# Layer 1's queries and output projections as single products of 128 array columns

## The chip, the cores and the metric

The kernel runs on one core of a Trainium2 chip. The metric is the device time of one execution in microseconds, taken several times; times are compared by their median. A profile is one more execution, recorded by the hardware profiler: every instruction with its engine, its start and its length. The engines are TensorE (PE; its weight loads are listed apart as PEld), VectorE (DVE), ScalarE (ACT), GpSimd (POOL) and SyncE (SP), whose queue issues most of the DMAs.

## What is computed

Two post-norm transformer layers over 8 sequences of 512 tokens with 512 features, all in f32. The part that matters here is the attention of layer 1, with 8 query heads of 64 features and 2 heads of keys and values:

```python
h = norm_scale * x / (nrm + EPS) * split_scale
q = (h @ Wq.T).reshape(b, s, H, dh)          # H = 8, dh = 64
k = (h @ Wk.T).reshape(b, s, G, dh)          # G = 2
v = (h @ Wv.T).reshape(b, s, G, dh)
...
scores = jnp.einsum('bghsd,bgtd->bghst', q, k) / np.float32(np.sqrt(dh))
attn = jax.nn.softmax(scores, axis=-1)
out = jnp.einsum('bghst,bgtd->bghsd', attn, v)
out = out.reshape(b, H, s, dh).transpose(0, 2, 1, 3).reshape(b, s, H * dh)
return x + out @ Wo.T
```

Ahead of it stand layer 0's causal attention with 16 heads and a mixture of 8 experts of which each token takes 2; behind it a gated feed-forward with integer weights of 1408 hidden units. A layer norm follows each of the four parts. The change touches layer 1's attention alone.

## The kernel before

The program runs in four stages: layer 0's attention, the experts' tiles (128 tokens each), layer 1's attention, layer 1's feed-forward. All 8 sequences ("batches" b) go through one stage before the next one begins, apart from a few pieces that are drawn forward at the seams.

Layer 1's attention is the class `Attention1`. A batch is held turned, features on the partitions: `hT` is 128 partitions by 4 blocks c of 128 features by 512 tokens. The query heads are paired, one head of each group of keys beside one of the other: a pair g (of 4) has 2 x 64 = 128 columns. The pieces of work, with the lines that the profile names them by:

- `key`, `value` (L1746, L1754): the 128 columns of both heads' keys or values. The results are `ps_k` and `ps_v`.
- `query(g)` (L1763): the 128 columns of the pair g, four products over the feature blocks c, summed in one PSUM bank `ps_q`, and a copy by ScalarE to `qT` (L1770).
- `score` (L1869): for 128 keys at a time, the scores of both heads of a pair against 512 queries (`sc`), four products with 64 rows and 64 columns; ScalarE then writes the exponentials `p` (L1876).
- `product` (L1888): `p` with the values, summed over the four blocks of keys in `av` (L1895); one product of 64 columns for each head.
- `normalise` (L1900): the sums over the keys by a product with ones, `rs` (L1903), then ScalarE's copy (L1081), VectorE's reciprocal (L1906) and multiplication (L1913) into `aoT`, the attention's turned result.
- `project(b, t)` (L1835) and `project_groups` (L1841): the output projection of 128 tokens t, four products over the pairs of heads, into `ps_o`; VectorE adds it to the stream (L1848).

The products of keys, values, queries and outputs all go through `multiply` (L1713), which hands them to `matmul_by_columns` (L61). That one cuts a product of 128 columns of weights into products of `columns` columns each, which write their own part of the partitions of the result; every one of them reads the whole moving operand. All instructions that it makes have the line L65 in the profile, so the tile's name (`ps_q`, `ps_o`, `ps_k`, `ps_v`, `sc`) tells them apart. The first argument of `multiply` chooses: where it is zero (or false) the product stays whole, with 128 columns; else it is cut in two of 64. Keys and values pass b, queries `b or g`, outputs 1. So before the change only batch 0's keys, values and the query of its pair 0 are whole.

A product of f32 operands in the program stands as two instructions on TensorE, each with its weight load.

The order of the work is written out: `batches` (L1808) takes, for each batch, eight slots from `plan` (L1916). In each slot TensorE gets the scores of two units (a unit is a pair g and a block of keys), then the pieces that the plan has put there (queries, keys, values, outputs of the batch before, transposes), then `product` for the two units of the slot before, and after every fourth unit `normalise`. TensorE, VectorE, ScalarE and GpSimd run their instructions in this order (`in_order`, L68), and the DMAs of this stage are issued from the same pieces. Queries come in slots 0, 1, 3 and 7 in the middle batches (slot 7's is the first of the next batch, behind its values), outputs in slots 2 to 5. Batch 7 has in four slots a piece that turns a block of batch 0 for the feed-forward with transposes (`ps_xT`, L1196). After the last slot come batch 7's own outputs: the first three products of token block 0, `rs`, three products of each of the other token blocks, and the fourth products of all four, each followed by VectorE's L1848. Then the feed-forward begins with `ps_g` (L1231); its banks were in part those of the scores and outputs.

Of the kernel before, what the change touches and what calls it, by code (L numbers as in the profile page):

```python
# [18 lines left out]
P = 128  # L19
# [1674 lines left out]
class Attention1:  # L1694
# [21 lines left out]
    def prepare(self, b):  # L1716


        nc, own, w_qkv = self.nc, self.own, self.w_qkv
        st = self.state[b] = {"qT": [None] * ND}  # L1720
        combine = Combine(self.router, b, self.rows, ("rows0", "rows1"))

        def norm():
            st["xn"], st["scale"] = combine.norm()

        def turn(c):
            if c == 0:
                st["hT"] = own.tile([P, ND, S], F32, tag="hT", name="hT1")
            ps = self.mm([P, S], "ps_hT")
            for t in range(NT):  # L1730
                nc.tensor.transpose(ps[:, ts(t, P)], st["xn"][:, t, ts(c, P)], self.env.ident)
            nc.scalar.copy(st["hT"][:, c, :], ps)

        def blocks(t):
            if t == 0:
                st["room"] = self.rows.tile([P, ND * S], F32, tag="rows1", name="turned")
            self.turn.blocks(st["room"], t, st["xn"][:, t, :])
            if t == NT - 1:
                self.turn.out(st["room"])
                st["hT"] = own.tile([P, ND, S], F32, tag="hT", name="hT1")  # L1740
                back = self.turn.back(st["hT"].rearrange("p k s -> p (k s)"))
                if 2 <= b < NB - 1:
                    with self.env.tc.issue_after(back.ins):
                        self.load_rows(b + 1)

        def key():  # L1746
            hT = st["hT"]
            ps = self.mm([P, S], "ps_k1")
            for c in range(ND):
                self.multiply(b, ps, w_qkv[:, 4, ts(c, P)], hT[:, c, :], c)  # L1750
            st["kT"] = own.tile([P, S], F32, tag="kT", name="kT", bufs=2)
            nc.scalar.copy(st["kT"], ps)

        def value():  # L1754
            hT = st["hT"]
            ps = self.mm([P, NT, P], "ps_v1")
            for t in range(NT):
                for c in range(ND):
                    self.multiply(b, ps[:, t, :], hT[:, c, ts(t, P)], w_qkv[:, 5, ts(c, P)], c)
            st["v"] = own.tile([P, NT, P], F32, tag="v", name="v1", bufs=2)  # L1760
            nc.scalar.copy(st["v"], ps)

        def query(g):  # L1763

            hT = st["hT"]
            ps = self.mm([P, S], "ps_q1")
            for c in range(ND):
                self.multiply(b or g, ps, w_qkv[:, c, ts(g, P)], hT[:, c, :], c)
            st["qT"][g] = (self.work if g % 2 else own).tile([P, S], F32, tag="qT", name="qT")
            nc.scalar.copy(st["qT"][g], ps)  # L1770

        return {"fetch": combine.fetch, "add": combine.add, "sum": combine.sum, "stat": combine.stat, "deviations": combine.deviations, "norm": norm,
                "turn": turn, "blocks": blocks, "key": key, "value": value, "query": query}
# [34 lines left out]
    def batches(self, work, p_sc, p_av, weights, split):  # L1808
        env, nc, guard, state, HD = self.env, self.nc, self.guard, self.state, self.HD
# [6 lines left out]
        w_out = work.tile([P, ND, 512], F32, name="attn1_out")  # L1816
# [18 lines left out]
        def project(b, t):  # L1835
            ps = self.mm([P, D], "ps_o1")
            project_groups(b, t, ps, range(ND))
            residual(b, t, ps)
            statistics(b, t)

        def project_groups(b, t, ps, groups):  # L1841
            for c in groups:
                self.multiply(1, ps, state[b]["aoT"][:, c, ts(t, P)], w_out[:, c, :], c)

        def residual(b, t, ps):
            st = state[b]
# [22 lines left out]
        def score(b, g, kt):  # L1869
            st = state[b]  # L1870
            sc = p_sc.tile([P, 2, S], F32, tag="sc", name="sc1")
            for j in range(2):
                hs = slice(HD * j, HD * (j + 1))
                matmul_by_columns(nc, sc[:, j, :], st["kT"][hs, ts(kt, P)], st["qT"][g][hs, :], columns=HD)
            p = work.tile([P, 2, S], F32, tag="p", name="p1", bufs=4)
            nc.scalar.activation(p, sc, AF.Exp, scale=scale)  # L1876
            return p
# [87 lines left out]
        for b in range(NB):  # L1965
            for i, thunks in enumerate(plan(b)):
                units = [(b, u // NT, u % NT) for u in (2 * i, 2 * i + 1)]
                ps = [score(*unit) for unit in units]
# [12 lines left out]
        b = NB - 1  # L1981
        banks = [self.mm([P, D], "ps_o1")]
        project_groups(b, 0, banks[0], range(ND - 1))
        sums[-1]()
        prepare_table(AF.Silu)
        banks += [p_sc.tile([P, 2, S], F32, tag="sc", name="ps_o1")[:, 1, :] for _ in range(2)]
        banks.append(self.mm([P, D], "ps_o1"))
        for t in range(1, NT):
            project_groups(b, t, banks[t], range(ND - 1))
# [360 lines left out]
```

## Time and profile before

| | us |
|---|---|
| three runs | 2099.91, 2100.9, 2104.41 |
| their median | 2100.9 |
| the profiled execution | 2098.14 |
| its span, first to last instruction | 2096.2 |
| TensorE busy in the span | 2072.5 |
| VectorE, ScalarE, GpSimd busy | 1275.9, 606.8, 503.3 |

By stage, in us of the span:

| stretch | what | TensorE busy | VectorE busy |
|---|---|---|---|
| 0 to 716 | layer 0's attention, first tiles of the experts | 707.9 | 488.1 |
| 716 to 1057 | the experts' tiles | 339.8 | 110.5 |
| 1057 to 1600 | layer 1's attention | 540.9 | 428.2 |
| 1600 to 2096 | the feed-forward | 483.9 | 249.1 |

How to read a line of the groups: line of the kernel, engine, operation, result<-operands, rows\*columns of the array, shape and type of the moving operand, number of instructions, then busy time in us and the mean length of one in ns, and the idle time of the engine just before them. A line of the timeline has the start and the length of a merged run of instructions in us, then the same names and their number. Two matmuls on different columns of the array run side by side, so the busy time of a pair is that of one. The length of a single matmul includes its way through the array; what a stream of them costs is the distance of their starts.

### The profile page before, as it was taken

The page shows a single profiled execution, that of the slowest core. Times are in us where ns is not written, and L with a number is a line of the kernel's source. Part 1 is how long each engine was busy: PE and PEld are TensorE (multiplying, and loading weights), DVE is VectorE, ACT ScalarE, POOL GpSimd, SP SyncE. Part 2 cuts the span into 40 slices and gives each one's busy share as a digit, 9 for nine tenths or more (in the row PEclk, how much of TensorE's full clock was granted, in tenths as well). Part 3 has the DMA queues.
Part 4 walks back from the last instruction along what each step waited for, and adds up shares of the span by engine and source line. Part 5 has one row for each costly group of instructions (what it writes and reads, how often), then busy time and mean ns, then how long its engine had stood idle before and what let it go on. Part 6 is the DMA issues. An engine that isn't in the chain of part 4 may idle for free. (4 is left out here: it accounts for less than half of the span.)

```text
span 2096.2 us, 35861 instructions
## 1 busy us (share of the span) xinstructions
PE 2072.5 (99%) x15074; PEld 1048.4 (50%) x15074; DVE 1275.9 (61%) x1965; ACT 606.8 (29%) x840; POOL 503.3 (24%) x509
## 2 busy tenths in 40 slices
PE   9999999999999999999999999999999999999998
PEld 2333333333334677774433333333335888888886
DVE  2667776777768633234157888887868644455444
ACT  2333433324333111111143333333332322222222
POOL 1343444434433221221052231222101000000000
PEclk9999999999999999999999999999999999999999
DMA  9011304324233568876431332233102311111000
GB/s 327 22 46 57 102 16 117 122 70 154 82 102 112 171 200 256 243 225 203 148 101 51 121 111 81 66 106 101 41 1 71 101 41 61 61 61 61 20 21 22
DMA packets 182090, 213.39 MB, mean 102 GB/s; under 512 B 72586, under 2 KB 126090, under 8 KB 178850
## 3 DMA queue, kind: packets, MB, share of 16 engines
q1 hardware_dynamic: 169280, 172.85, 26.3%
q0 software_dynamic: 10560, 34.61, 5.7%
q10 hardware_dynamic: 2082, 3.56, 0.6%
q8 instruction: 121, 1.98, 0.4%
q14 instruction: 47, 0.39, 0.1%
HBM read 132.58 MB, written 78.40 MB: 101 GB/s over the span
## 5 line engine op out<-in xcount | busy, mean ns | idle before, releaser
L1492 ACT ACTIVATE p<-sc 128x2048 f32<-128x2048 f32 (+1 forms) x96 | 153.1, 1595 | 172.0 <-PE sc L65 148.3
L1236 DVE SCALAR_TENSOR_TENSOR hT<-ps_u,vec,sg 128x512 f32<-128x512 f32 x88 | 65.5, 745 | 190.1 <-PE ps_u L1231 189.9
L1084 POOL TENSOR_TENSOR g_total<-g_total,r_inv 128x512 f32<-128x512 f32 x64 | 90.7, 1417 | 351.8 <-DVE r_inv L1906 270.8
L1247 PE MATMUL ps_f<-ffn_w,h_half 128*128 128x512 f32 x664 | 167.7, 393 | 2.7 <-DVE h_half L1242 2.0
L964 PE MATMUL ps_gu<-xrT,experts 128*128 128x256 f32 x736 | 166.6, 379 | 0.0
L964 PEld LDWEIGHTS ps_gu<-xrT,experts 128*128 128x128 f32 x736 | 139.3, 190 | 35.9 <-issue 19.3
L1539 DVE TENSOR_TENSOR p<-p 128x1536 f32<-128x1536 f32 (+2 forms) x96 | 136.5, 1422 | 32.6 <-PE av L1531 17.6
L1502 POOL TENSOR_SCALAR_AFFINE_SELECT p<-p 128x512 f32<-128x512 f32 x128 | 84.4, 672 | 290.7 <-ACT p L1492 287.6
L1876 ACT ACTIVATE p<-sc 128x1024 f32<-128x1024 f32 x128 | 124.2, 1022 | 100.3 <-PE sc L65 99.0
L1906 DVE RECIPROCAL r_inv<-r_inv 128x512 f32<-128x512 f32 x32 | 107.1, 3347 | 72.7 <-ACT r_inv L1081 72.7
L1247 PEld LDWEIGHTS ps_f<-ffn_w,h_half 128*128 128x128 f32 x664 | 122.9, 188 | 34.4 <-DVE h_half L1242 7.3
L1231 PE MATMUL ps_g<-x_high,ffn_w 128*128 128x512 f32 x352 | 137.2, 390 | 0.0
L1231 PE MATMUL ps_g<-x_low,ffn_w 128*128 128x512 f32 x352 | 137.0, 389 | 0.0
L1231 PE MATMUL ps_u<-x_high,ffn_w 128*128 128x512 f32 x352 | 137.0, 389 | 0.0
L1231 PE MATMUL ps_u<-x_low,ffn_w 128*128 128x512 f32 x352 | 137.0, 389 | 0.0
L65 PE MATMUL sc<-qT,kT 64*64 64x512 f32 x1024 | 124.7, 602 | 1.2 <-ACT qT L1770 0.9
L65 PE MATMUL ps_q<-experts 128*32 128x512 f32 x1024 | 121.2, 602 | 4.7 <-DMA experts<-in_xT 4.4
L65 PE MATMUL ps_v<-experts 128*32 128x512 f32 x1024 | 120.9, 594 | 0.0
L1895 PE MATMUL av<-p,v 128*64 128x512 f32 x512 | 120.8, 593 | 0.0
L1234 ACT ACTIVATE sg<-ps_g,vec 128x512 f32<-128x512 f32 x88 | 60.6, 689 | 195.4 <-PE ps_g L1231 195.4
L65 PE MATMUL ps_o<-attn_out,aoT 128*64 128x512 f32 x512 | 116.4, 598 | 0.0
L65 PE MATMUL ps_k<-experts 128*32 128x512 f32 x1024 | 116.3, 594 | 0.0
(280 smaller groups left out, 3270.3 us busy)
## 6 DMA issues: line engine op xcount, KB each, us to landing
results<-y SPq DMA_DIRECT2D x68, 256.0 KB, 2.9
pair<-xrT SPq DMA_DIRECT2D x30, 512.0 KB, 3.0
xrT<-pair SPq DMA_DIRECT2D x120, 128.0 KB, 3.9
turned<-turned SPq DMA_DIRECT2D x56, 256.0 KB, 4.1
x<-in_x SPq DMA_DIRECT2D x8, 1024.0 KB, 8.5
rows<-x SPq DMA_DIRECT2D x32, 256.0 KB, 2.1
experts<-in_xT SPq DMA_DIRECT2D x7, 1024.0 KB, 11.8
x<-rows SPq DMA_DIRECT2D x14, 512.0 KB, 6.6
```

The lines of the kernel that those rows point to most:

```text
L65: nc.tensor.matmul(out[m], lhsT=lhsT[:, m], rhs=rhs, start=start, stop=stop)
L964: nc.tensor.matmul(ps[:, j, :], lhsT=w, rhs=xT[:, c, :], start=c == 0, stop=c == ND - 1)
L1084: self.nc.gpsimd.tensor_tensor(self.total, self.total, r_inv, ALU.add)
L1231: nc.tensor.matmul(ps, lhsT=w[:, ts(dc, P)], rhs=x[:, dc, :], start=(dc, i) == (0, 0), stop=(dc, i) == (ND - 1, 1))
L1236: nc.vector.scalar_tensor_tensor(hT, u, vec[:, V_SU + c : V_SU + c + 1], sg, ALU.mult, ALU.mult)
L1247: self.nc.tensor.matmul(os[t], lhsT=h[:, ts(t, P)], rhs=self.weights(2 * NHID + c), start=(c, i) == (0, 0), stop=(c, i) == (NHID - 1, 1))
L1492: nc.scalar.activation(p, sc[:, :, :width], AF.Exp, scale=scale)
L1502: select = nc.gpsimd.affine_select(out=first, in_=first, pattern=[[0, 4], [1, P]], compare_op=ALU.is_ge, fill=0.0, base=0, channel_multipl ...
L1539: nc.vector.tensor_tensor(total[:, :, P * kt :], total[:, :, P * kt :], p[:, :, at : at + w], ALU.add)
L1876: nc.scalar.activation(p, sc, AF.Exp, scale=scale)
L1895: nc.tensor.matmul(st["av"][HD * j : HD * (j + 1), :], lhsT=st["v"][:, kt, HD * j : HD * (j + 1)], rhs=p[:, j, :], start=kt == 0, stop=kt ...
L1906: nc.vector.reciprocal(r_inv, r_inv)
```

## The change

Queries and output projections pass 0 to `multiply` in place of `b or g` and 1. Each of their products is then a single one of 128 columns that reads its moving operand once; the results, their banks and the places in the order stay as they are. Keys and values are still cut in two for the batches after 0, the scores and the products with `p` and ones are as before.

```diff
@@ -1765,7 +1765,7 @@
             hT = st["hT"]
             ps = self.mm([P, S], "ps_q1")
             for c in range(ND):
-                self.multiply(b or g, ps, w_qkv[:, c, ts(g, P)], hT[:, c, :], c)
+                self.multiply(0, ps, w_qkv[:, c, ts(g, P)], hT[:, c, :], c)
             st["qT"][g] = (self.work if g % 2 else own).tile([P, S], F32, tag="qT", name="qT")
             nc.scalar.copy(st["qT"][g], ps)
 
@@ -1840,7 +1840,7 @@
 
         def project_groups(b, t, ps, groups):
             for c in groups:
-                self.multiply(1, ps, state[b]["aoT"][:, c, ts(t, P)], w_out[:, c, :], c)
+                self.multiply(0, ps, state[b]["aoT"][:, c, ts(t, P)], w_out[:, c, :], c)
 
         def residual(b, t, ps):
             st = state[b]
```

## The prediction

> **What bounds the kernel now.** I read the page first (engines, clock, chain), then the busy time by stage, then what TensorE waits for in the stage that the change touches, and last the order of its work in time.
>
> ```profile
> PE 2072.5 (99%) x15074; PEld 1048.4 (50%) x15074; DVE 1275.9 (61%) x1965; ACT 606.8 (29%) x840; POOL 503.3 (24%) x509
> ...
> PEclk9999999999999999999999999999999999999999
> ```
>
> TensorE is busy all the time, at the full granted clock. Layer 1's attention is the stretch from 1057 to 1600 us:
>
> ```profile
> 1057.00:1600.00 543.00, 540.92 (x3274) 182.57 (x3273) 428.22 (x479) 180.93 (x251) 145.72 (x132) 1.00 0.25 75
> ```
>
> 540.9 of 543 us are TensorE's, VectorE has 428 and the others far less. From the first product that changes (1065.7 us) to the end of the stage TensorE waits for another engine twice, 0.9 us in all, both times around the transposes of batch 0:
>
> ```profile
> PE ps_hT L1731 <- ACT hT L1732: 0.7, 1, 0.7
> PE ps_k L65 <- ACT hT L1732: 0.2, 1, 0.2
> ```
>
> So in this stage every nanosecond added to or taken from TensorE's stream goes to the end. The groups that change, and the one query that already is a single product (batch 0, group 0):
>
> ```profile
> L65 PE MATMUL ps_o<-attn_out,aoT 128*64 128x512 f32 x512 | 116.4, 598 | 0.0
> L65 PE MATMUL ps_q<-hT,attn_qkv 128*64 128x512 f32 x496 | 112.6, 596 | 0.0
> ...
> L65 PE MATMUL ps_q<-hT,attn_qkv 128*128 128x512 f32 x8 | 3.6, 592 | 0.0
> ```
>
> "128*64" is rows times columns of the array. Each f32 product of the program is two instructions, so a query of 4 products is 16 as pairs (8 waves of two) and 8 as single ones. Now time, as start, length, what:
>
> ```profile
> 1121.86 1.89 PE L1895 MATMUL av<-p,v 128*64 128x512 f32 x8
> 1123.58 1.03 PE L1903 MATMUL rs<-total,ones 128*64 128x512 f32 x4
> 1124.53 1.95 PE L65 MATMUL sc<-qT,kT 64*64 64x512 f32 x16
> 1126.41 3.65 PE L65 MATMUL ps_q<-hT,attn_qkv 128*64 128x512 f32 x16
> 1129.90 1.89 PE L1895 MATMUL av<-p,v 128*64 128x512 f32 x8
> 1131.71 1.95 PE L65 MATMUL sc<-qT,kT 64*64 64x512 f32 x16
> 1133.59 1.94 PE L65 MATMUL ps_o<-attn_out,aoT 128*64 128x512 f32 x8
> ```
>
> The products av (4 waves) take 1.72 us from their start to that of rs, 0.43 a wave (0.429 from the single starts). From av to the scores it is 1.81, 0.10 more; the scores' 4 waves take 1.88, 0.16 more. A change of the array's form costs time; a change of operands does not (av to rs, both 128\*64). Three places show the form 128\*128:
>
> ```profile
> 1055.20 1.98 PE L989 MATMUL ps_y<-experts,hT 128*128 x4 [0.52 <-ACT hT L983]
> 1057.02 3.60 PE L65 MATMUL ps_q<-hT,attn_qkv 128*128 128x512 f32 x8
> ```
>
> ```profile
> 1527.72 1.03 PE L65 MATMUL ps_q<-hT,attn_qkv 128*64 128x512 f32 x4
> 1528.68 0.66 PE L1196 MATMUL ps_xT<-ident,x 128*128 128x128 f32 x4
> 1529.27 1.94 PE L1895 MATMUL av<-p,v 128*64 128x512 f32 x8
> ```
>
> ```profile
> 715.08 1.45 PE L989 MATMUL ps_y<-experts,h 128*128 128x512 f32 x3
> 716.46 1.07 PE L505 MATMUL ps_logits<-x1T,r_wr 128*32 128x512 f32 x8
> 717.45 1.35 PE L964 MATMUL ps_gu<-xrT,experts 128*128 128x256 f32 x5
> ```
>
> **The prices, in ns, from the starts of single instructions in this trace.** A wave of 512 columns takes 429 in every form (the single query: 3.60 = 7 x 0.429 + 0.592). A change of form has two parts.
> - Leaving a form stretches its last wave: leaving 64\*64 by 110 (539 for 429, 18 queries and 28 outputs; 111 into 128\*128, where the scores stand before a transpose), leaving 128\*64 by 100 (529; 101 into 128\*128), leaving 128\*128 by 93 (ps_y to ps_logits 522 for 429; ps_xT to av 202 for 109, four times of four).
> - In the new form the first weights are not loaded ahead: the first wave is longer by 24 where they have 32 columns (ps_logits, 453), by 51 with 64 (480), by 104 with 128 (ps_y after the idle time, 533; ps_gu after ps_logits 320 for 216). Transposes, with 128 columns, show 57 (166 for 109).
>
> **The change part by part.**
>
> Waves. 31 queries and 32 output projections (28 inside the loop, 4 at its end) are 504 waves, pairs before and single instructions after. The step is 429 in both forms, so the 504 matmul and 504 weight-load instructions that go away free no time. Nearest rows allow 1 ns either way: bounds -0.5 and +0.5 us, taken 0.
>
> Changes of form. TensorE, VectorE, ScalarE and GpSimd run in program order here, and only the form of these products changes, no place. After each block of scores come the queries or outputs of that slot, then av and often rs, which stay 128\*64, then scores. Now one change leads into the 128\*64 run and one back; after the change a 128\*128 run stands between:
> - Scores to a query or output, 28 + 18 = 46 times: 111 + 104 in place of 110 + 51, 54 more: **+2.5 us**. Bounds by the load's rows, 57 (transposes) and 104: +0.3 and +2.5; 104, as these are f32 products like ps_y and ps_gu.
> - From the query or output back to the pairs, new: 30 times to av after a query, 20 after an output, once to rs: 51. Each 93 + 51 = 144: **+7.3 us**. The transition of a 512-column product into 128\*64 is not in the trace; its halves are (ps_y's exit, av's entry), and ps_xT to av is the whole at 128 columns. Bounds: 117 (the whole of ps_y to ps_logits) and 151 (128\*64 to scores), +6.0 and +7.7.
> - From pairs into a single product, new: seven times from the values to a query in one slot, and twice in the last batch's end (av to output, rs to output): 9 x (101 + 104) = **+1.8 us**; bounds 158 (into a transpose) and 217 (ps_logits to ps_gu), +1.4 and +2.0.
> - Gone: query to ps_xT once, output to ps_xT twice, in batch 7: 3 x (101 + 57) = **-0.5 us**.
> - The last output to the feed-forward's ps_g changes form no more, but ps_g's first weights wait for VectorE's third residual there (L1848, ends at 1599.76, ps_g starts at 1599.81; without the form change it could start 1599.65). 0; at best -0.2.
>
> Sum: 2.5 + 7.3 + 1.8 - 0.5 = **+11.2 us**; the bounds together +6.5 to +12.2.
>
> Other engines. No instruction of VectorE, ScalarE, GpSimd or any DMA is added, removed or moved, and each change shows as TensorE arriving later, which gives the others more slack. The two waits of 0.9 us in batch 0 follow ScalarE's copies of transposes that TensorE itself has just made, so they move along and hide nothing; the 3.0 us that TensorE idles in the feed-forward stage lie behind its own products in the same way. If they hid all, 3.9 us would be off.
>
> Where a rule differs from the rows. The Trainium skill, "TensorE: Matmul & The Clock Gate", Part 3, The mechanism, says that a weight load overlaps running matmuls only if it goes to other row groups. All 128 rows are in use in both forms here; by that rule each wave would show its load, 104 in place of 51, and the sum would have some 27 us more. The rows have 429 for both forms, load hidden, so I leave it out. "TensorEngine Tiling (Array Packing)", Gotcha 2, says that column tiling excludes the fast weight load; a reader may conclude that undivided products load faster. With the transposes' 57 in place of 104, 55 entries cost 2.6 us less and the sum is +8.6; ps_y and ps_gu, undivided f32, show 104.
>
> **The rivals.**
> - *Forms of 128 rows count as one.* If 128\*128 and 128\*64 follow each other freely, only the scores' entries (+2.5) and the lost transposes (-0.5) remain: +2.0 us, which cannot be told from no change; this is the case that ends not slower. For it: av to rs to outputs cost nothing. Against: ps_xT to av, and query to ps_xT. It decides where the exit and the entries from pairs cost under (4.2 - 2.0) / 60 = 37 ns each, against 144 and 205 in the rows.
> - *The single wave is faster*, as half the instructions and half the reading of the moving operand go. It takes back the 11.2 us at 11.2 / 504 = 22 ns a wave, and ends faster by 0.2% (4.2 us) from 31 ns on; at 395 ns a wave it would be -5.9 us. Against: 429 for the single query, for 30 of 31 steps in layer 0's undivided outputs and for ps_y.
> - *Weights of 128 columns show in every wave* when the engines around are busy: 504 x 53 = +27 us on top, +38. Against: the same rows; but the single query ran with other work thin.
> - That the change does nothing is out: the built program has 8 instructions per query for 16, and as many changes of form as counted.
>
> **How the numbers follow.** Chances: my forecast 0.86, forms as one 0.06, faster wave 0.03, loads showing 0.05. The profiled execution took 2098.1 us (span 2096.2 and 1.9 around it), 2.8 below the median of the three runs, 2100.9; the middle of the four is 2100.4. The forecast is 2098.1 + 11.2 = 2109.3 on the profile's own scale and 2100.4 + 11.2 = 2111.6 for a median. Its bounds, +6.5 to +12.2, give 2106.9 to 2112.6, and the runs before spread 4.5 us, mostly upwards; with 0.07 of the chance left out on each side the range is 2106.5 to 2117. 0.2% is 4.2 us, about what a measurement can tell: slower (over 2105.1) holds the forecast and the showing loads, 0.91 and a little more from the spread; same is most of forms as one and a little of the second, 0.06; faster 0.02.
>
> **What would show it.** Right: TensorE 504 matmuls fewer; ps_q and ps_o as 128\*128 with starts 429 apart; the first such wave after scores 533; 51 last waves of 522 before av or rs, and 480 after; the stage some 11 us longer and everything outside it unchanged. Wrong: 429 from ps_q to av (forms as one), steps under 410 (faster wave) or near 530 throughout (loads show), or new waits of TensorE for another engine.

## The result, and the profile after

The changed kernel takes 2109.88 us (median of 6 runs, 2108.80 to 2110.84) against 2100.40 of the kernel before (6 runs, 2098.04 to 2104.41): a ratio of 1.0043, 95% interval 1.0032 to 1.0054. It is slower. The profiled executions differ by more: 2108.80 to 2098.14 us, spans 2107.1 to 2096.2, 10.9 us. In the later comparisons the kernel before had medians of 2099.3, 2098.6 and 2098.9 us over 15 to 21 runs; against those the difference is 10.6 to 11.3 us as well. So the median of 2100.40 lay a little high.

The page of the changed kernel, its engines and clock:

```profile
PE 2083.2 (99%) x14570; PEld 1067.0 (51%) x14570; DVE 1275.9 (61%) x1965; ACT 606.6 (29%) x840; POOL 502.8 (24%) x509
...
PEclk9999999999999999999999999999999999999999
```

TensorE has 504 instructions fewer and is busy 10.7 us longer; the busy times of the other engines are the same within 0.5 us. By stage (busy time of TensorE, its weight loads, VectorE, ScalarE, GpSimd; then clock, DMA):

```profile
0.00:716.00 716.00, 707.73 (x8488) 250.83 (x8488) 488.34 (x814) 239.31 (x275) 282.71 (x287) 1.00 0.34 108
716.00:1057.00 341.00, 339.76 (x1203) 220.23 (x1202) 110.69 (x257) 55.04 (x107) 59.97 (x63) 1.00 0.68 201
1057.00:1611.00 554.00, 551.92 (x2770) 201.67 (x2769) 427.76 (x479) 180.77 (x251) 145.66 (x132) 1.00 0.24 73
1611.00:2107.00 496.00, 483.75 (x2114) 394.31 (x2113) 249.15 (x417) 131.52 (x207) 14.41 (x27) 0.99 0.17 55
```

All of it lies in the third stretch, layer 1's attention: 554 us with 551.9 of TensorE for 543 with 540.9. The stretches ahead of it and behind it are as before to 0.2 us of TensorE. From its first changed product on, TensorE waits for the same two things in it, for as long as before:

```profile
PE ps_hT L1731 <- ACT hT L1732: 0.7, 1, 0.7
...
PE ps_k L65 <- ACT hT L1732: 0.2, 1, 0.2
```

So no new wait took the time. The groups have the new form, half as many instructions, and are a little longer in busy time (ps_o 117.9 for 116.4):

```profile
L65 PE MATMUL ps_o<-attn_out,aoT 128*128 128x512 f32 x256 | 117.9, 604 | 0.0
L65 PE MATMUL ps_q<-hT,attn_qkv 128*128 128x512 f32 x256 | 117.7, 602 | 0.0
```

The same place of the timeline as shown of before, with the values of the slot ahead of it:

```profile
1108.11 3.71 PE L65 MATMUL ps_v<-attn_qkv,hT 128*64 128x128 f32 x64
1111.75 3.70 PE L65 MATMUL ps_q<-hT,attn_qkv 128*128 128x512 f32 x8
...
1125.49 1.95 PE L65 MATMUL sc<-qT,kT 64*64 64x512 f32 x16
1127.36 3.70 PE L65 MATMUL ps_q<-hT,attn_qkv 128*128 128x512 f32 x8
1130.99 1.94 PE L1895 MATMUL av<-p,v 128*64 128x512 f32 x8
1132.86 1.95 PE L65 MATMUL sc<-qT,kT 64*64 64x512 f32 x16
1134.74 3.70 PE L65 MATMUL ps_o<-attn_out,aoT 128*128 128x512 f32 x8
```

From the query's start to that of av it is 3.63 us where it was 3.49, and from av to the scores 1.87 where it was 1.81. Together 0.20 us a slot. From the scores' start to the query's it is 1.88 us in both: the change is in what follows them.

### The profile page after: what moved, and what is told of

It is laid out like the page before. It is cut to its first block, busy times and chain, and to the rows that moved or that the text cites. A ratio compares the mean times of both kernels' runs of the same rounds, so it can differ in the third digit from the quotient of the medians.

```text
span 2107.1 us, 34839 instructions
## 1 busy us (share of the span) xinstructions
PE 2083.2 (99%) x14570; PEld 1067.0 (51%) x14570; DVE 1275.9 (61%) x1965; ACT 606.6 (29%) x840; POOL 502.8 (24%) x509
## 5 line engine op out<-in xcount | busy, mean ns | idle before, releaser
L65 PE MATMUL ps_o<-attn_out,aoT 128*128 128x512 f32 x256 | 117.9, 604 | 0.0
L65 PE MATMUL ps_q<-hT,attn_qkv 128*128 128x512 f32 x256 | 117.7, 602 | 0.0
```

The lines of the kernel that those rows point to most:

```text
L65: nc.tensor.matmul(out[m], lhsT=lhsT[:, m], rhs=rhs, start=start, stop=stop)
```

## The experiments

Two theories stood after the result. A: the array pays for every change of its form, by the prices of the prediction. B: each single wave costs a little more, 10.9 us over 504 waves, 22 ns each. (A wave is one single product, or the two, four or eight cut ones that run side by side.) The trace of the changed kernel speaks for A (steps of 429 inside a run), and the runs test it by the number of changes. Since executions start layer 1's attention between 1056.5 and 1058.9 us, whatever the kernel, each is measured by its stage: from the first query to the feed-forward's first ps_g, 1057.02 to 1599.81 before (542.80 us) and 1056.94 to 1610.78 after (553.84, **11.05 more**). The expectations name the span instead. By spans the differences lie from 0.6 us below to 2.0 us above those of the stage, because the rest of the program, which no edit touches, varies.

| kernel | theory A, us on the stage of before | measured stage, us | difference | median, us | ratio, 95% interval |
|---|---|---|---|---|---|
| changed kernel | +11.2 | 553.84 | +11.05 | 2109.88 | 1.0043 [1.0032, 1.0054] |
| queries alone | +7.8 | 550.47 | +7.68 | 2105.86 | 1.0030 [1.0019, 1.0041] |
| outputs alone | +5.5 | 548.25 | +5.46 | 2103.47 | 1.0021 [1.0011, 1.0031] |
| first half of each output | +6.9 | 549.73 | +6.93 | 2105.61 | 1.0029 [1.0018, 1.0040] |
| every other product of each output | +17.4 | 560.17 | +17.38 | 2115.84 | 1.0076 [1.0059, 1.0092] |
| fewer slots, single products | +7.6 and waits | 563.81 | +21.01 | 2119.48 | 1.0101 [1.0087, 1.0116] |
| fewer slots, pairs | 0.0 and waits | 556.27 | +13.48 | 2111.65 | 1.0062 [1.0048, 1.0077] |
| keys and values single too | +11.7 | 554.73 | +11.94 | 2110.47 | 1.0058 [1.0042, 1.0073] |
| 32 columns everywhere | -1.8 to -2.7 | 543.17 | +0.37 | 2098.34 | 0.9998 [0.9989, 1.0007] |
| 32 columns, scores 64 | -0.9 | 542.00 | -0.80 | 2097.95 | 0.9997 [0.9987, 1.0006] |

**Queries alone, outputs alone.** Each takes one line of the change.

```diff
-                self.multiply(b or g, ps, w_qkv[:, c, ts(g, P)], hT[:, c, :], c)
+                self.multiply(0, ps, w_qkv[:, c, ts(g, P)], hT[:, c, :], c)
```

> Queries are single products of 128 columns, outputs stay pairs. Theory A (price per change of the array's form: leaving 64*64 110, 128*64 100, 128*128 93 ns, plus the first load of 51 or 104 ns): 17 slots with a query alone cost 198 ns each, 7 with values ahead of the query and 6 with an output ahead of it 349 each, and the query ahead of a transpose saves 104: +7.8 us on the span of before (2096.2). Theory B (each single wave costs the same bit more, 10.9 us / 504 waves = 22 ns): 248 waves, +5.4 us.

```diff
-                self.multiply(1, ps, state[b]["aoT"][:, c, ts(t, P)], w_out[:, c, :], c)
+                self.multiply(0, ps, state[b]["aoT"][:, c, ts(t, P)], w_out[:, c, :], c)
```

> Outputs are single products, queries stay pairs. Theory A: 25 runs at 198 ns, two ahead of transposes that save 104 each, and 0.75 us at the end of batch 7: +5.5 us on the span of before. With the queries alone that makes 13.3 us, 2.1 more than the 11.2 of both together, since in six slots an output and a query stand side by side and then share their changes of form. Theory B: 256 waves, +5.6 us, and the two add up to both.

Measured +7.68 and +5.46 us. The nearly equal numbers of waves (248 and 256) cost unequal times, as A has it, and the two together are 13.14, 2.09 more than both at once: in six slots an output and a query share their changes. B gives 5.4 and 5.6 and a plain sum.

**Half of the products.** The outputs' four products in two kinds, once two and two, once in turn.

```diff
-                self.multiply(1, ps, state[b]["aoT"][:, c, ts(t, P)], w_out[:, c, :], c)
+                self.multiply(c // 2, ps, state[b]["aoT"][:, c, ts(t, P)], w_out[:, c, :], c)
```

> Of each output's four products the first two are single, the last two pairs; queries stay pairs. Half of the single waves of outputs alone, but as many runs of them, and two transposes that are no longer reached in the same form. Theory A: 28 runs at 198 ns and 1.4 us at the end of batch 7: +6.9 us on the span of before, more than with all four single. Theory B: 128 waves, +2.8 us.

```diff
-                self.multiply(1, ps, state[b]["aoT"][:, c, ts(t, P)], w_out[:, c, :], c)
+                self.multiply(c % 2, ps, state[b]["aoT"][:, c, ts(t, P)], w_out[:, c, :], c)
```

> Of each output's four products the first and third are single, the second and fourth pairs; queries stay pairs. As many single waves as with the first two single, but two more changes of form in each output. Theory A: 28 outputs at 198 + 349 = 547 ns and 2.1 us at the end of batch 7: +17.4 us on the span of before. Theory B: 128 waves, +2.8 us, as with the first two single.

Measured +6.93 and +17.38 us. Half the single waves cost more than all of them, and the same half costs two and a half times as much when the two kinds alternate. B is out: what is paid for is the change. In the timelines an output of the first kind (first line, 1143.67 to 1147.35) and one of the second (below, 1143.04 to 1147.07); the merged lines show the form of their first instruction, and 12 instructions are 4 single and 8 in pairs. The first view ends inside the query, hence 14 instructions for 16:

```profile
1143.67 3.85 PE L65 MATMUL ps_o<-attn_out,aoT 128*128 128x512 f32 x12
1147.35 3.17 PE L65 MATMUL ps_q<-hT,attn_qkv 128*64 128x512 f32 x14
```

```profile
1143.04 4.20 PE L65 MATMUL ps_o<-attn_out,aoT 128*128 128x512 f32 x12
1147.07 3.60 PE L65 MATMUL ps_q<-hT,attn_qkv 128*64 128x512 f32 x16
```

3.68 and 4.03 us for the same eight waves, 0.35 apart: one change into 128\*128 (205) and one out of it (144).

**Fewer slots.** If a run of single products costs some 198 ns however long it is, longer and fewer runs should cost less. The same edit of the plan was made in the changed kernel and in the kernel before:

```diff
-                for t, i in enumerate((2, 3, 4, 7) if final else (2, 3, 4, 5)):
+                for t, i in enumerate((2, 3, 4, 7) if final else (2, 2, 4, 4)):
...
-            for g, i in zip((1, 2, 3), (1, 3, 5) if first else (0, 1, 5) if final else (0, 1, 3)):
+            for g, i in zip((1, 2, 3), (1, 3, 5) if first else (0, 1, 5) if final else (1, 2, 4)):
```

> The changed kernel with its pieces put into fewer slots: in batches 1 to 6 the three queries of pairs 1 to 3 go to slots 1, 2 and 4 (before 0, 1 and 3) and the four outputs to slots 2, 2, 4, 4 (before 2 to 5), so that two outputs and a query stand side by side twice. All products are as many and as single as in the changed kernel. Theory A: three runs of single products fewer in each of six batches, 18 x 198 ns = 3.6 us less than the changed kernel, +7.6 us on the span of before; if the third product of such a slot has to wait for VectorE to free one of the two banks, that much more, and the waits of TensorE show it. Theory B (every single wave costs 22 ns): +11 us as the changed kernel.

> The kernel before with the same places of the queries and outputs, all of them in pairs: what the places alone do. Theory A: no change of form is added or taken away, as every slot has scores and products of p anyway: 0.0 us on the span of before. If the places themselves cost or bring time (banks, latency of ScalarE's copies), it shows here, and the comparison with the single products in the same places, 7.6 us by theory A, stays clean.

Both took some 13 us more than expected. The single products cost 7.54 us more than the pairs in the same places (563.81 to 556.27), 7.6 by A: three runs fewer in each batch do save what was counted. But the places cost far more than they save, +13.48 us in pairs already, where the expectations had named a wait for a bank and put no time on it. What TensorE waits for in the stage, and one of the places, in the kernel with pairs:

```profile
PE ps_q L65 <- DVE x L1848: 10.7, 6, 1.8
```

```profile
1149.43 7.09 PE L65 MATMUL ps_o<-attn_out,aoT 128*64 128x512 f32 x32
1158.31 3.65 PE L65 MATMUL ps_q<-hT,attn_qkv 128*64 128x512 f32 x16 [1.79 <-DVE x L1848]
```

The query is the third product in a slot and the banks are two; it waits until VectorE has read the first output, six times 1.8 us. With single products it is the same wait, 10.5 us. By the distance of starts, the six steps from an output to the query make up 11.8 of the 13.5 us in pairs; a wait is counted from the end of the last product, a step from its start. The steps from av to rs, which come later, make up 1.2, and first loads that show once more the rest.

**Keys and values too.**

```diff
-                self.multiply(b, ps, w_qkv[:, 4, ts(c, P)], hT[:, c, :], c)
+                self.multiply(0, ps, w_qkv[:, 4, ts(c, P)], hT[:, c, :], c)
...
-                    self.multiply(b, ps[:, t, :], hT[:, c, ts(t, P)], w_qkv[:, 5, ts(c, P)], c)
+                    self.multiply(0, ps[:, t, :], hT[:, c, ts(t, P)], w_qkv[:, 5, ts(c, P)], c)
```

> The changed kernel with layer 1's keys and values as single products too, so that only the scores, the products with p and those with ones are still cut. Theory A: six keys alone in a slot are six more runs of single products, 198 ns each, +1.2 us; the seven entries from values to a query go (205 each, -1.4), the seven entries from scores to values load 104 in place of 51, +0.4; the values' waves of 128 columns step 112 ns in place of 109 (batch 0's do), 217 of them, +0.6: +0.7 us on the changed kernel, its stage 554.5 us long for 553.8. Theory B (22 ns for every single wave, of 429 or of 109): 48 + 224 waves more, +6 us.

Measured 0.89 us more than the changed kernel, 0.7 by A and 6 by B. The values' waves step 112 or 111 ns for 109 before, as batch 0's had shown. Making everything single that can be does not bring the form changes down, because the products with p and with ones, two heads with different operands, stay cut.

**32 columns.** If the first load goes by its columns, a finer cut should pay less. Queries, outputs, keys, values, and the products with p and with ones are cut in four; once the scores too.

```diff
-        matmul_by_columns(self.nc, out, lhsT, rhs, c == 0, c == ND - 1, self.HD if b else P)
+        matmul_by_columns(self.nc, out, lhsT, rhs, c == 0, c == ND - 1, 32 if b else P)
...
-                matmul_by_columns(nc, sc[:, j, :], st["kT"][hs, ts(kt, P)], st["qT"][g][hs, :], columns=HD)
+                matmul_by_columns(nc, sc[:, j, :], st["kT"][hs, ts(kt, P)], st["qT"][g][hs, :], columns=32)
...
-                nc.tensor.matmul(st["av"][HD * j : HD * (j + 1), :], lhsT=st["v"][:, kt, HD * j : HD * (j + 1)],
-                                 rhs=p[:, j, :], start=kt == 0, stop=kt == NT - 1)
+                for at in range(HD * j, HD * (j + 1), 32):
+                    nc.tensor.matmul(st["av"][at : at + 32, :], lhsT=st["v"][:, kt, at : at + 32],
+                                     rhs=p[:, j, :], start=kt == 0, stop=kt == NT - 1)
...
-                nc.tensor.matmul(rs[HD * j : HD * (j + 1), :], lhsT=ones, rhs=total[:, j, :], start=True, stop=True)
+                for at in range(HD * j, HD * (j + 1), 32):
+                    nc.tensor.matmul(rs[at : at + 32, :], lhsT=ones[:, :32], rhs=total[:, j, :], start=True, stop=True)
```

> The other way: in layer 1's attention all products that are pairs of 64 columns before (keys, values, queries, outputs, scores, the products with p and with ones) are cut into 32 columns, four side by side; the scores have 64 rows and 32 columns. As many changes of form as before. Theory A: 128 entries load 32 columns in place of 64, 27 ns less each, -3.5 us; leaving 128*32 takes 113 ns by layer 0 in place of 100, 65 times, +0.8 us; leaving 64*32 is not shown, 110 to 125 ns, 0 to +0.9 us: -1.8 to -2.7 us on the span of before. Rival: four times the instructions of a single product are too many for a wave of 429 ns, or for the values' waves of 109 ns: then the steps between waves grow (the values' alone by up to 7 x 32 x 0.1 = 24 us). If finer cuts cost by themselves, it is slower than before.

The time is that of the kernel before (2098.34 to 2098.55 us). The starts say why the forecast of -1.8 to -2.7 was missed. The first waves take 453 in place of 480, as foreseen, and the steps stay 429, and 109 for the values, with four times the instructions of a single product. But leaving 64\*32 stretches the last wave to 566, 137 ns, where 110 to 125 were allowed for: a slot's two changes are 137 + 24 + 113 + 24 = 298 for 312, a saving of 0.9 us over 62 slots. In this execution it is covered by a wait for VectorE of 1.0 us in batch 0, which no other run of the study shows. One of the twelve executions of this kernel took 5525 us; its cause stays open.

The second kernel is the same without the second of the four edits, so that the scores keep their 64 columns.

> As with 32 columns everywhere, but the scores keep 64 rows and 64 columns. Theory A with the prices measured so far (leaving 64*64 110, 128*32 113; first load of 32 columns 24, of 64 columns 51): each slot's two changes 110 + 24 + 113 + 51 = 298 ns for 312 before, 62 times, -0.9 us on the stage of before (542.8), not to be told apart by the median. Rival: the finer cut of the products with 128 rows makes its own steps longer: steps over 429.

The timeline of this kernel, the scores, a query and the products with p:

```profile
1125.13 1.95 PE L65 MATMUL sc<-qT,kT 64*64 64x512 f32 x16
1127.01 3.64 PE L65 MATMUL ps_q<-hT,attn_qkv 128*32 128x512 f32 x32
1130.47 1.90 PE L1896 MATMUL av<-p,v 128*32 128x512 f32 x16
1132.30 1.95 PE L65 MATMUL sc<-qT,kT 64*64 64x512 f32 x16
```

From the query to av it is 3.46 us here, 3.49 in pairs and 3.63 with single products: three forms, the same eight waves, and 24, 51 and 104 + 93 ns around them. The stage is 0.80 us shorter than before for 0.9 foreseen; by the medians it cannot be told from the kernel before. No version of the study is measurably faster than the kernel before.

## Why the prediction was right

The prediction said slower, 2111.6 us (2106.5 to 2117.0), by +11.2 us of changes of form on a stream that nothing else delays. Term by term, from the starts in the changed kernel's trace:

- *Waves*: 429 in both forms, 0 as taken.
- *Scores to a single product*: the last wave of the scores 539 or 540, the first of the query or output 533 or 534 for 480: 53 x 46 = 2.4 us, foreseen 2.5.
- *Back to pairs*: 522 or 523 before av or rs in all 51 places, and 480 after: 144 x 51 = 7.3 us, as foreseen. This transition was not in the trace of before as a whole; putting it together from ps_y's exit and av's entry held to a nanosecond.
- *From pairs into a single product*: values to query 209 for 109, then 533; av and rs to an output 530 and 529, then 533: 204 x 9 = 1.8 us, as foreseen.
- *Gone at the transposes*: 429 before them and 109 as their first step: 3 x 158 = -0.5 us, as foreseen.
- *The last output to ps_g*: 572 for 590. It still waits for VectorE's third residual; 0 was right.

That is 11.1 us, measured 11.05 on the stage. The step that was a little off is none of these but the base: the sum was put on the middle of the four times shown, 2100.4, though the sum's own scale, the profiled execution, gave 2109.3 for a measured 2108.8. The forecast for the median lay 1.7 us too high. Beside the six runs of the kernel before, whose median is that same 2100.40, the change comes out as 9.5 us; beside the later medians of 2098.6 to 2099.3, which put the base 1.1 to 1.8 us lower, as 10.6 to 11.3.

Of the rivals, the one that counted forms of 128 rows as one fell with the 522 and the 480; the faster wave and the showing loads fell with the 429. Loads of 128 columns stay hidden behind running f32 products of all 128 rows also with VectorE and ScalarE at work beside them, which was the doubt left about the single query. The weight loads show it as well: inside a run of single products, from the third on, a load starts 1 or 2 ns behind the start of the product before, some 427 ns ahead of its own. One statement of the Trainium skill ("TensorE: Matmul & The Clock Gate", Part 3, The mechanism), that loads overlap only across row groups, is by itself not what these runs show; the same section also names a background weight buffer as a way to load ahead. The prediction's price for showing loads, 27 us, was wrong by its own rows: it counted 53 ns a wave, as if the pairs showed their 51, but the pairs step 429 with nothing showing. With 104 in each of the 449 single waves that are not the first of a run, the stage would by estimate be 47 us longer still, which puts that rival further from the measured time. The undivided products did not load faster either, as one might conclude from "TensorEngine Tiling (Array Packing)", Gotcha 2: 104 ns for their first load at 55 entries, by the columns.

## What to carry to other kernels

Where TensorE's stream is the path, two forms with the same step are not equal: count the places where the array's rows or columns change from one instruction to the next, and price each as the stretch of the last wave before it plus the first load after it. A product that fills the array by itself can lose to two halves if its neighbours are halves. The price is per run, not per product, but runs can be merged only as far as the banks allow, and a wait of 1.8 us for a bank eats nine saved runs.

## What had not been expected

- Leaving a form costs more the finer it is cut: 93 ns for 128\*128, 100 for 128\*64, 110 for 64\*64, 113 for 128\*32, 137 for 64\*32 (565 or 566 for 429 in 60 of the 61 places of that run where scores lead into 128\*32). Where nothing else is waited for, it does not depend on the form that comes next beyond 2 ns.
- Behind these five prices stands nearly one. The instructions of a wave start 6 to 7 ns apart, so the last of one, two, four or eight starts 0, 7, 20 or 47 ns after the first. Counted from that last start, the next form begins 522 to 524 ns later behind every form of 128 rows and 519 or 520 behind those of 64 rows (traces of the kernel before, the changed one and 32 columns everywhere). So leaving costs 93 ns, or 90 with 64 rows, and the finer cut adds the spread of its last wave.
- The first load after a change goes by its columns, 24, 51 and 104 ns for 32, 64 and 128, while f32 transposes, also with 128 columns, show 57. In the traces of the kernel before, the changed one and 32 columns everywhere, the first load behind each change of form starts only 1 to 3 ns ahead of its product.
- These prices added up to within 0.25 us of the measured stage in every kernel without a new wait, from -0.8 to +17.4 us, on a program of 2100 us.
